# Layer 0 of a four-layer graph kernel: two expert blocks from the first token group, and first products ahead of the last gates

## The chip, the cores and the metric

The kernel runs on one core of a Trainium2 chip. The metric is the device time of one execution in microseconds (us). A forecast and a result are compared by the median of several executions. The engines are TensorE (PE, with PEld for its weight loads), VectorE (DVE), ScalarE (ACT), GpSimd (POOL) and SyncE (SP), which issues most DMAs; each works through its own queue in order.

## The reference

There are 2708 tokens of 256 features. Each of four layers first mixes tokens through an adjacency matrix and then applies a feed-forward part; the change is in layer 0:

```python
x = x + weights(adj) @ (layernorm(x) @ W + B)   # weights: exp(-2 (1/adj - 1)^2) where adj < 1, else 0
xf = layernorm(x)
gate_logits = xf @ Wg + bg                      # 8 experts
top_w, top_i = jax.lax.top_k(gate_logits, 2)    # two experts for each token
top_w = jax.nn.softmax(top_w, axis=-1)
for e in range(8):
    h = gelu(xf @ W1[e] + b1[e])                # 256 -> 1024
    out = out + w_dense[:, e:e+1] * (h @ W2[e] + b2[e])   # 1024 -> 256
x = x + out
```

## The kernel before

Tokens are cut in 22 tiles of 128 rows (the last one has 20), and the tiles in three groups, `GROUPS`: tiles 0 to 8, 9 to 15 and 16 to 21. For each group the kernel makes the **sums** of the mixing step. A loop over `j` loads one row block of the transposed adjacency matrix, as wide as the group (`adrow`, five buffers, on SP's queue); `weigh` turns it into weights with three ScalarE and two VectorE instructions (`wt`, four buffers); TensorE multiplies them with the messages `msg` (L893) into PSUM. When a group's sums are done, VectorE adds them to `x` (L916), and `send` takes the group's tokens through the **gates**. It normalises rows (`stats`, `norm_to`, L187), turns them on TensorE (`turn_to`, L203) and copies them on ScalarE (L204), multiplies by `Wg` (L807), finds the two best experts and their weights (`top2_weights`), works out a place in an expert-sorted list for each of a token's two copies (`route`, L384 to L402) and scatters the copies there with indirect DMAs on GpSimd (L492, into the DRAM tensor `taken0`). Each expert has one part of the list for each group, since a group's counts are known only after its gates. Of the next group's sums, as much as fits lies beside a group's gates.

The **expert blocks** then take 256 list entries of one expert at a time. `blocks` computes on VectorE, from the counts that are known (`known`), which expert (`ei`) and which list entries (`ix`) each block has. Full blocks that the first two groups are certain to fill are called "A" (`NA = 9`), and are found before the last group's gates; "B" and "C" are found after them. `took` says how many full blocks of each expert were used, so that later calls leave them out. An object of class `Blocks` runs them. `fetch` reads the expert's number into a register of SP and loads its weights, `wa` and `wb` (L761, L766); `fetch_rows` gathers the rows (L506, `xs`), behind all scatters that may have written them; `turn` transposes them (L558) and copies them on VectorE (L564, `xTs`). `run` then makes the first products (L591, four instructions for each of 8 slices of the hidden layer), Gelu on ScalarE (L593, `hTs`), the second products (L601, into `yacc`), adds the bias and multiplies by the gate's weight on VectorE (L603, L604), and scatters the result (L492, `given`). There are 24 such blocks in this stage.

The order of work on each engine is made when the program is built: a planner takes the instructions in the order of the program text, puts one that is ready ahead of an earlier one that is not, and adds the waits. The text adds orders of its own where wanted. In the kernel before, the first block's turn is put behind the gates' product of the third-last tile:

```python
work0.run(hc, items, beside, gated[-3])
```

The two first blocks' rows are fetched in the text near the end of the last group's loop (`j == NT - 5`), behind the scatters of the first and the second group, and their weights after that loop:

```python
if end and j == NT - 5:
    past = list(scattered["taken0"])
    items = [(full, b, past, taken[0][: 2 * held], True) for b in range(NA)]
```

Weights are loaded behind the last matrix row that was asked for in the text at that point (`reads[-1]`). The PSUM banks and the SBUF pools of the blocks (`hc`) take the place of those of the sums, tile by tile. The last group's `stats` go by Ln and Exp on ScalarE (`by_log`), those of the other groups by a square root in integer and float steps on VectorE (`rsqrt`, L152 to L163).

Of the kernel before, what the change touches and what calls it, by code (L numbers as in the profile page):

```python
# [36 lines left out]
def rows(t):  # L37
    return min(P, N - t * P)
# [28 lines left out]
def adj_ffn4(ctx: ExitStack, tc: tile.TileContext, a: dict, out: bass.AP):  # L67
# [24 lines left out]
    def ps_acc():  # L92
        return pools["psum"].tile([P, W], F32, tag="acc", name="ps_acc", bufs=pools["acc"])
# [311 lines left out]
    def blocks(pool, brief, known, NB, B, name, done=None, full=False, least=0):  # L405
# [44 lines left out]
        ei = pool.tile([P, NB], I32, name="b_ei", tag="b_ei" + name)  # L450
        v.tensor_scalar(ei, eb[:, :, 0], float(E - 1), None, op0=ALU.min)
        v.tensor_tensor(vec[:, 0, :], nb[:, :, 0], end, ALU.subtract)
        if done is not None:
            v.tensor_tensor(vec[:, 0, :], vec[:, 0, :], done, ALU.add)
        v.tensor_tensor(hot, eb.to_broadcast([P, NB, E]),
                        count[:, None, :E].to_broadcast([P, NB, E]), ALU.is_equal)
        part = brief.tile([P, NB, K, E], F32, name="b_part", tag="b_part" + name, bufs=1)
# [9 lines left out]
        row = pool.tile([P, NB, M], F32, name="b_row", tag="b_row" + name)  # L467
        step = pool.tile([P, NB, M], F32, name="b_step", tag="b_step" + name)
        ix = pool.tile([P, NB, M], I32, name="b_ix", tag="b_ix" + name)
        v.tensor_tensor(row, pos, of[:, :, 1:2].to_broadcast([P, NB, M]), ALU.add)  # L470
        for i in range(1, len(known) - 1):

            v.tensor_tensor(step, pos, of[:, :, 2 * i : 2 * i + 1].to_broadcast([P, NB, M]), ALU.is_ge)
# [1 line left out]
                            ALU.mult)  # L475
            v.tensor_tensor(ix if full and i == len(known) - 2 else row, row, step, ALU.add)
        if full:

            took = pool.tile([P, E], F32, name="b_took")
            v.tensor_scalar(took, vec[:, 0, :], float(NB), None, op0=ALU.add)  # L480
            v.scalar_tensor_tensor(took, took, 0.0, nb[:, :, 0], op0=ALU.max, op1=ALU.min)
# [41 lines left out]
    class Blocks:  # L523
# [4 lines left out]
        def __init__(self, pool, given, weights):  # L528
            self.pool, self.given = pool, given
            self.weights, self.ahead, self.rows, self.at = weights, [], [], [0, 0]  # L530
            self.late = None
            self.ik, self.ok = "taken0", "given0"

        def fetch(self, item):
# [14 lines left out]
                gather(xs[:, k, :], src, ix[:, b, k : k + 1], src.shape[0] - 1, self.ik, past)  # L549
            self.rows.append((xs, ix.shape[2]))  # L550

        def turn(self, pool, rows, after=None):
            xs, n = rows
            xT = pool.tile([P, DC, 2 * P], F32, name="xTs", bufs=2)
            p = pools["psum"].tile([P, W], F32, name="turned", bufs=1)
            for k in range(n):
                for c in range(DC):
                    i = te.transpose(p[:, (c * 2 + k) * P : (c * 2 + k + 1) * P],  # L558
                                     xs[:, k, c * P : (c + 1) * P], ident)
                    if after is not None:  # L560
                        tc.add_manual_dep(i.ins, after, mybir.DependencyInfo(
                            mybir.DependencyClass.NoSync, mybir.DependencyReason.DATA),
                            reason="order")
            v.tensor_copy(xT[:, :, : n * P], p.rearrange("p (c t) -> p c t", c=DC)[:, :, : n * P])  # L564
            return xT

        def run(self, pool, items, during=None, after=None):

            HC = 1024 // P
            self.late = pool  # L570
            ahead, todo, rows_todo = self.ahead, list(items[len(self.ahead):]), list(items[len(self.rows):])
            while rows_todo and len(self.rows) < 3:
                self.fetch_rows(rows_todo.pop(0))
            while todo and len(ahead) < 2:
                self.fetch(todo.pop(0))
            turned = self.turn(pool, self.rows[0], after)
            for n in range(len(items)):
                w1, bias, w2 = ahead.pop(0)
                (xs, m), xT = self.rows.pop(0), turned
                if rows_todo:  # L580
                    self.fetch_rows(rows_todo.pop(0))
# [4 lines left out]
                hT = pool.tile([P, HC, 2 * P], F32, name="hTs", bufs=1)  # L586
                for f in range(HC):
                    if f % 2 == 0:
                        p = ps_acc().rearrange("p (k t) -> p k t", k=2)
                    for c in range(DC):  # L590
                        te.matmul(p[:, f % 2, : m * P], lhsT=w1[:, c, f * P : (f + 1) * P],  # L591
                                  rhs=xT[:, c, : m * P], start=(c == 0), stop=(c == DC - 1))
                    s.activation(hT[:, f, : m * P], p[:, f % 2, : m * P], AF.Gelu,  # L593
                                 bias=bias[:, f : f + 1])
                if self.rows:
                    turned = self.turn(pool, self.rows[0])
                y = pool.tile([P, 2, D], F32, name="ys", bufs=2)
                q = pools["psum"].tile([P, 2, D], F32, name="yacc", bufs=2)
                for k in range(m):
                    for f in range(HC):  # L600
                        te.matmul(q[:, k, :], lhsT=hT[:, f, k * P : (k + 1) * P], rhs=w2[:, f, :],  # L601
                                  start=(f == 0), stop=(f == HC - 1))
                    v.tensor_tensor(y[:, k, :], q[:, k, :], w2[:, HC, :], ALU.add)  # L603
# [146 lines left out]

    NA, MOST = 9, (2 * N + E * (P - 1)) // (2 * P)
    assert NA <= -(-(2 * held - E * (2 * P - 1)) // (2 * P))
    ALWAYS, HALVES = 13, 2
    with ExitStack() as l0:
        hw = l0.enter_context(tc.tile_pool(name="h0", side="right", reuse_waits="tile", bufs=1))
# [14 lines left out]
        hcs, reads, gated, own_rows = [], [], [], []  # L770
# [15 lines left out]
        def send(tiles):  # L786
# [4 lines left out]
            if tiles is GROUPS[-1]:  # L791
                parts = [tiles[:2], tiles[2:]]
            st = {t: (z, t - part[0]) for part in parts
                  for z in [stats(part, by_log=len(parts) > 1)] for t in part}
            xr = (tp if len(parts) == 1 else own_rows[0]).tile(
                [P, GMAX if len(parts) == 1 else G, 2, XW], F32, name="xr", bufs=1)[:, :G]
            lg = tp.tile([P, G, E], F32, name="lg", tag=f"lg{G}", bufs=1)
# [1 line left out]
            for i, t in enumerate(tiles):  # L799
                r = rows(t)  # L800
                norm_to(xr[:r, i, 0, :D], t, st[t][1], st[t][0])
                g.tensor_copy(xr[:r, i, 1, :D], xr[:r, i, 0, :D])
                xT = tp.tile([P, DC, P], F32, name="xT", bufs=2)
                turn_to(xT[:, :, :r], xr[:r, i, 0, :D], r, ps_acc() if len(parts) > 1 else None)
                p = ps_tmp()
                for c in range(DC):
                    made = te.matmul(p[:r, :E], lhsT=xT[:, c, :r], rhs=wg[:, c, :],  # L807
                                   start=(c == 0), stop=(c == DC - 1))
                gated.append(made.ins.name)
# [43 lines left out]
        for tiles in GROUPS:  # L853
# [8 lines left out]
            for j in range(FULL):  # L862
# [33 lines left out]
                if end and j == 2:  # L896
                    cols = [gp.tile([P, GMAX * P], F32, name=name, tag=name, bufs=bufs)[
                        :, : NT * Q].rearrange("p (t c) -> p t c", c=Q)
                            for name, bufs in (("adrow", 5), ("y", 3), ("wt", 4))]
                    last_columns(cols[0])  # L900
                    weigh(*cols, P)
                    last = last_sums(acc[-1].rearrange("p k d -> p (k d)"), cols[2],
                                     lambda j, r: msg[:r, j, :], D)
                    v.tensor_tensor(x[:LAST, FULL, :], x[:LAST, FULL, :], last, ALU.add)
                if end and j == NT - 5:
                    past = list(scattered["taken0"])
                    items = [(full, b, past, taken[0][: 2 * held], True) for b in range(NA)]
                    for item in items[:2]:
                        work0.fetch_rows(item)
            for item in items[:2] if end else ():  # L910
                work0.fetch(item)
            for p, pair in zip(acc, pairs):
                if pair[0] == len(own):
                    continue
# [2 lines left out]
            if end:  # L917
# [5 lines left out]
                hcs.append(hc)  # L923
                own_rows.append(behind_gate.enter_context(
                    tc.tile_pool(name="x0", reuse_waits="tile", bufs=1)))
            send(tiles)
            if tiles is GROUPS[-2]:
                full = blocks(hw, tp, known, NA, 2 * P, "A", full=True)
        rest = blocks(hw, hc, known, MOST - NA, 2 * P, "B", done=full[2], least=P)
        twice = hw.tile([P, E], F32, name="twice")  # L930
        v.tensor_tensor(twice, full[2], rest[3], ALU.add)
# [39 lines left out]
                    ad[: rows(j)], a["adjT"][j * P : j * P + rows(j), c0 : c0 + N // 2]))  # L971
                read.append((j, c0, ad))

        work0.run(hc, items, beside, gated[-3])
        assert not parts and not read
        work0.run_rest(hc, more, left[0])

# [927 lines left out]
```

## Time and profile before

| | us |
|---|---|
| median of 3 runs | 1936.62 |
| lowest and highest | 1930.79, 1938.07 |
| the profiled execution | 1935.32 |
| its span, first to last instruction | 1933.6 |

| engine | busy us | share of the span | instructions |
|---|---|---|---|
| PE | 1827.5 | 95% | 9453 |
| DVE | 1092.7 | 57% | 2439 |
| ACT | 642.1 | 33% | 1461 |
| POOL | 344.5 | 18% | 405 |

The profile is one execution. A matrix product in float32 stands in it as two instructions. Its views are a page with the busy share of each engine in 40 equal slices, windows with busy times and the granted TensorE clock (1.00 is full speed), a timeline of each engine, and lists of who waited for whom: a wait is put down to the releaser that came last. In layer 0 the second group's sums end about 197, the third group's at 257, and the expert blocks last until about 607 us.

### The profile page before, as it was taken

The numbers are of one execution on the slowest core, as the hardware profiler recorded it, in microseconds if no ns is written. First come the engines' busy times: TensorE is split into PE (matmuls) and PEld (weight loads), VectorE is DVE, ScalarE is ACT, GpSimd is POOL, SyncE is SP. The second block draws the span as 40 slices with busy tenths as digits, with TensorE's granted clock in tenths as the row PEclk, the third lists the DMA queues.
The fourth block names the chain that finished last, engine by engine and source line by source line (L and its number), as shares of the span: only waits on it lengthen the run. The fifth ranks groups of instructions, "written<-read, shape, count | busy, mean of one in ns | idle before, by whom it ended". The sixth has DMA issues, their size and how long they took to land.

```text
span 1933.6 us, 25684 instructions
## 1 busy us (share of the span) xinstructions
PE 1827.5 (95%) x9453; PEld 1327.0 (69%) x9453; DVE 1092.7 (57%) x2439; ACT 642.1 (33%) x1461; POOL 344.5 (18%) x405
## 2 busy tenths in 40 slices
PE   7999989999998999999796799999899999999998
PEld 6888778888887888888676678888557732232344
DVE  7776862444333524444441175555354398999897
ACT  7868732222223303122231142223232552031131
POOL 1005263333321002314336300000000000000000
PEclk9999989999998999999898999999899999999999
DMA  8435476887764454535777620000101000000000
GB/s 274 138 114 155 120 273 243 342 311 282 301 254 133 144 151 118 149 106 131 222 243 262 264 75 1 1 1 1 44 1 33 17 1 23 23 12 28 20 20 15
DMA packets 90141, 243.94 MB, mean 126 GB/s; under 512 B 18159, under 2 KB 44823, under 8 KB 80792
## 3 DMA queue, kind: packets, MB, share of 16 engines
q1 hardware_dynamic: 70048, 197.09, 30.9%
q0 software_dynamic: 16960, 42.42, 6.9%
q10 hardware_dynamic: 3000, 2.70, 0.5%
q8 instruction: 78, 1.28, 0.3%
q14 instruction: 55, 0.45, 0.1%
HBM read 216.29 MB, written 28.71 MB: 127 GB/s over the span
## 4 chain that ended last, share of the span: by engine, by line
PE 73%; DMA 12%; DVE 6%; issue 5%; ACT 2%; POOL 2%; SPq 0%; POOLq 0%; DVEq 0%; ACTq 0%
PE num L1803 10%; PE ps_acc L1382 9%; PE acc L1174 8%; PE ps_tmp L357 7%; PE acc L893 7%; PE den L1813 6%; PE ps_acc L591 5%; PE yacc L601 4%; PE ps_tmp L250 4%; DMA given<-ys,xs 4%; PE ps_acc L1566 3%; PE yacc L693 2%; DMA hs<-hid,names 2%; DMA given<-ys,names 1%; PE ps_tmp L203 1%
## 5 line engine op out<-in xcount | busy, mean ns | idle before, releaser
L1773 DVE SCALAR_TENSOR_TENSOR e<-arena,G,mask 128x1024 f32<-128x1024 f32 (+1 forms) x264 | 287.0, 1149 | 13.6 <-PE den L1813 13.6
L1803 PE MATMUL num<-e,wh 128*64 128x512 f32 (+4 forms) x1056 | 215.8, 551 | 0.0
L1382 PE MATMUL ps_acc<-hh,e 128*128 128x257 f32 x882 | 199.2, 382 | 1.7 <-ACT o L1327 1.7
L893 PE MATMUL acc<-msg,wt 128*128 128x256 f32 x882 | 198.5, 382 | 2.0 <-DVE wt L851 1.2
L1174 PE MATMUL acc<-sup,adrow 128*128 128x256 f32 x882 | 198.6, 382 | 1.8 <-DVE adrow L1146 1.8
L893 PEld LDWEIGHTS acc<-msg,wt 128*128 128x128 f32 x882 | 165.6, 191 | 28.0 <-DVE wt L851 2.1
L1174 PEld LDWEIGHTS acc<-sup,adrow 128*128 128x128 f32 x882 | 165.1, 190 | 28.7 <-issue 5.2
L1382 PEld LDWEIGHTS ps_acc<-hh,e 128*128 128x128 f32 x882 | 163.7, 190 | 29.2 <-ACT o L1327 4.3
L591 PE MATMUL ps_acc<-xTs,wa 128*128 128x256 f32 (+1 forms) x768 | 170.6, 375 | 1.0 <-DVE xTs L564 0.8
L593 ACT ACTIVATE hTs<-ps_acc,wa 128x256 f32<-128x256 f32 (+1 forms) x192 | 88.6, 464 | 244.4 <-PE yacc L601 165.6
L601 PE MATMUL yacc<-wb,hTs 128*128 128x256 f32 x736 | 167.4, 380 | 1.9 <-DVE ys L603 1.9
L591 PEld LDWEIGHTS ps_acc<-xTs,wa 128*128 128x128 f32 x768 | 137.6, 191 | 27.3 <-DVE xTs L564 3.8
L1803 PEld LDWEIGHTS num<-e,wh 128*64 128x64 f32 (+1 forms) x1056 | 66.5, 136 | 127.3 <-issue 106.5
L601 PEld LDWEIGHTS yacc<-wb,hTs 128*128 128x128 f32 x736 | 137.6, 190 | 20.2 <-DVE ys L603 2.7
L1376 DVE SCALAR_TENSOR_TENSOR e<-Rb,G,mask 128x640 f32<-128x640 f32 (+2 forms) x110 | 85.1, 775 | 93.1 <-PE ps_acc L1382 93.0
L1813 PE MATMUL den<-e,wh 128*32 128x512 f32 (+4 forms) x1056 | 118.0, 548 | 0.0
L204 ACT COPY xT<-ps_tmp 128x256 f32<-128x256 f32 x98 | 33.6, 364 | 242.5 <-PE ps_tmp L203 217.2
L1143 DVE TENSOR_SCALAR mask<-adrow 128x1024 uint8<-128x1024 f32 (+1 forms) x66 | 41.7, 631 | 124.2 <-DMA adrow<-in_adjT 124.0
L693 PE MATMUL yacc<-wb,hTs 128*128 128x256 f32 x384 | 90.6, 387 | 0.3 <-DMA wb<-in_L_ffn_Wdp 0.3
L851 DVE SCALAR_TENSOR_TENSOR wt<-adrow,wt 128x640 f32<-128x640 f32 (+3 forms) x67 | 71.1, 1063 | 30.6 <-ACT wt L141 30.3
L1813 PEld LDWEIGHTS den<-e,wh 128*32 128x32 f32 (+1 forms) x1056 | 30.2, 108 | 77.9 <-issue 73.8
L492 POOL DMA_INDIRECT given<-ys,xs x46 | 65.9, 1432 | 83.7 <-DVE ys L604 77.9
(452 smaller groups left out, 2570.8 us busy)
## 6 DMA issues: line engine op xcount, KB each, us to landing
adhalf<-in_adjT SPq DMA_DIRECT2D x42, 677.0 KB
wb<-in_L_ffn_W2p SPq DMA_DIRECT2D x24, 1152.0 KB
wb<-in_L_ffn_Wdp SPq DMA_DIRECT2D x24, 1152.0 KB
wa<-in_L_ffn_W1b SPq DMA_DIRECT2D x24, 1028.0 KB
adrow<-in_adjT SPq DMA_DIRECT2D x42, 512.0 KB
adrow<-in_adjT SPq DMA_DIRECT2D x42, 320.0 KB
adrow<-in_adjT SPq DMA_DIRECT2D x21, 576.0 KB
adrow<-in_adjT SPq DMA_DIRECT2D x21, 448.0 KB
```

The source lines that it names most:

```text
L357: te.matmul(p[:, :w], lhsT=w1[:, c, f * P : (f + 1) * P], rhs=xnT[:, c, c0 : c0 + w], start=(c == 0), stop=(c == DC - 1))
L591: te.matmul(p[:, f % 2, : m * P], lhsT=w1[:, c, f * P : (f + 1) * P], rhs=xT[:, c, : m * P], start=(c == 0), stop=(c == DC - 1))
L593: s.activation(hT[:, f, : m * P], p[:, f % 2, : m * P], AF.Gelu, bias=bias[:, f : f + 1])
L601: te.matmul(q[:, k, :], lhsT=hT[:, f, k * P : (k + 1) * P], rhs=w2[:, f, :], start=(f == 0), stop=(f == HC - 1))
L693: te.matmul(q, lhsT=hT[:, f, :], rhs=w2[:, f, :], start=(f == 0), stop=(f == HC - 1))
L893: te.matmul(p[:q, n - pair[0], :], lhsT=wt[:, k : k + q], rhs=msg[:r, j, :], start=(j == 0 and n == pair[0]), stop=(j == FULL - 1 and n == ...
L1174: te.matmul(p[:q, n - pair[0], :], lhsT=ad[:, k : k + q], rhs=sup[:r, j, :], start=(j == 0 and n == pair[0]), stop=(j == FULL - 1 and n == ...
L1376: v.scalar_tensor_tensor(e[:r, :w], Rb[:r, c0 : c0 + w], G[:r, j, :], mask[:r, j, c0 : c0 + w], op0=ALU.max, op1=ALU.mult)
L1382: te.matmul(p[:, : D + 1], lhsT=e[:, k : k + q], rhs=hh[:, j, :], start=(j == 0), stop=False)
L1773: v.scalar_tensor_tensor(e[:, :w], slow[:, m % 2, k, :w], G[:, j, 2 * pair + k, :], mask[:, j, c0 : c0 + w], op0=ALU.max, op1=ALU.mult)
L1803: te.matmul(num[k * DK : (k + 1) * DK, hf, :q], lhsT=wh[some, j, 2 * pair + k, :DK], rhs=e[some, h0 - c0 : h0 - c0 + q], start=(j == 0), s ...
L1813: te.matmul(den[z : z + Q, :q], lhsT=wh[some, i, 2 * pair + k, DK : DK + 1] .to_broadcast([some.stop - some.start, Q]), rhs=e[some, h0 - c ...
```

## The change

There are now two "E" blocks (`N0 = 2`). By counting alone, the first group of 1152 tokens, with 2304 copies over 8 experts, has at least two full blocks of 256. They are found right after the first group's gates. Their rows are fetched at `j == 0` of the last group's loop, behind the first group's scatters alone; their weights at `j == 8` and `j == 14` of that loop. "A" has the seven others of the nine, and leaves out what "E" took.

When the last group's sums are done, the text goes on with the turn and the first products of the first block (`first_products`, cut out of `run`), and only then with the last group's gates, whose transposes are put behind the last one of these products (`at_last`). The last group's `stats` now go by `rsqrt` on VectorE as the others' do. The number of blocks and the work in them are the same. `took` moves up in `blocks` and is made before `done` is added.

```diff
@@ blocks
+        if full:
+            took = pool.tile([P, E], F32, name="b_took", tag="b_took" + name)
+            v.tensor_scalar(took, vec[:, 0, :], float(NB), None, op0=ALU.add)
+            v.scalar_tensor_tensor(took, took, 0.0, nb[:, :, 0], op0=ALU.max, op1=ALU.min)
         if done is not None:
             v.tensor_tensor(vec[:, 0, :], vec[:, 0, :], done, ALU.add)
+            if full:
+                v.tensor_tensor(took, took, done, ALU.add)
...
@@ class Blocks
-        def turn(self, pool, rows, after=None):
+        def turn(self, pool, rows):
...
+        def first_products(self, pool, weights, xT, m):
+            w1, bias, _ = weights
+            hT = pool.tile([P, HC, 2 * P], F32, name="hTs", bufs=1)
+            for f in range(HC):
+                if f % 2 == 0:
+                    p = ps_acc().rearrange("p (k t) -> p k t", k=2)
+                for c in range(DC):
+                    i = te.matmul(p[:, f % 2, : m * P], lhsT=w1[:, c, f * P : (f + 1) * P],
+                                  rhs=xT[:, c, : m * P], start=(c == 0), stop=(c == DC - 1))
+                s.activation(hT[:, f, : m * P], p[:, f % 2, : m * P], AF.Gelu,
+                             bias=bias[:, f : f + 1])
+            self.at_last = i.ins.name
+            return hT
...
-            turned = self.turn(pool, self.rows[0], after)
+            turned = self.begun or self.turn(pool, self.rows[0])
+            self.begun = None
...
+                hT = self.made or self.first_products(pool, (w1, bias, w2), xT, m)
+                self.made = None
...
@@ send
-                  for z in [stats(part, by_log=len(parts) > 1)] for t in part}
+                  for z in [stats(part)] for t in part}
...
+                first = len(nc.cur_bb.bb.instructions)
                 turn_to(xT[:, :, :r], xr[:r, i, 0, :D], r, ps_acc() if len(parts) > 1 else None)
+                for k in nc.cur_bb.bb.instructions[first:] if len(parts) > 1 else ():
+                    if k.engine == mybir.EngineType.PE:
+                        tc.add_manual_dep(k, work0.at_last, mybir.DependencyInfo(
+                            mybir.DependencyClass.NoSync, mybir.DependencyReason.DATA),
+                            reason="order")
...
@@ the loop of the sums
+                if end and j == 0:
+                    items = [(early, b, past0, taken[0][: 2 * held0], True) for b in range(N0)]
+                    for item in items:
+                        work0.fetch_rows(item)
+                if end and j in (8, 14):
+                    work0.fetch(items[j // 6 - 1])
                 if end and j == NT - 5:
                     past = list(scattered["taken0"])
-                    items = [(full, b, past, taken[0][: 2 * held], True) for b in range(NA)]
-                    for item in items[:2]:
-                        work0.fetch_rows(item)
-            for item in items[:2] if end else ():
-                work0.fetch(item)
+                    items += [(full, b, past, taken[0][: 2 * held], True) for b in range(NA - N0)]
...
+                work0.late = hc
+                work0.begun = work0.turn(hc, work0.rows[0])
+                work0.made = work0.first_products(hc, work0.ahead[0], work0.begun, 2)
             send(tiles)
+            if begin:
+                early = blocks(hw, tp, known, N0, 2 * P, "E", full=True)
+                past0 = list(scattered["taken0"])
             if tiles is GROUPS[-2]:
-                full = blocks(hw, tp, known, NA, 2 * P, "A", full=True)
+                full = blocks(hw, tp, known, NA - N0, 2 * P, "A", done=early[2], full=True)
...
-        work0.run(hc, items, beside, gated[-3])
+        work0.run(hc, items, beside)
```

More of the change, by code (lines that the diff above doesn't have):

```diff
@@ L469, in blocks @@
         ix = pool.tile([P, NB, M], I32, name="b_ix", tag="b_ix" + name)
-        v.tensor_tensor(row, pos, of[:, :, 1:2].to_broadcast([P, NB, M]), ALU.add)
+        v.tensor_tensor(ix if full and len(known) == 2 else row, pos,
+                        of[:, :, 1:2].to_broadcast([P, NB, M]), ALU.add)
         for i in range(1, len(known) - 1):
@@ L477, in blocks @@
         if full:
-            took = pool.tile([P, E], F32, name="b_took")
-            v.tensor_scalar(took, vec[:, 0, :], float(NB), None, op0=ALU.add)
-            v.scalar_tensor_tensor(took, took, 0.0, nb[:, :, 0], op0=ALU.max, op1=ALU.min)
             return ei, ix, took
@@ L530, in __init__ @@
             self.weights, self.ahead, self.rows, self.at = weights, [], [], [0, 0]
-            self.late = None
+            self.late, self.begun, self.made = None, None, None
             self.ik, self.ok = "taken0", "given0"
@@ L557, in turn, with run @@
                 for c in range(DC):
[L558 to L563, printed above, removed]
+                    te.transpose(p[:, (c * 2 + k) * P : (c * 2 + k + 1) * P],
+                                 xs[:, k, c * P : (c + 1) * P], ident)
             v.tensor_copy(xT[:, :, : n * P], p.rearrange("p (c t) -> p c t", c=DC)[:, :, : n * P])
             return xT
-        def run(self, pool, items, during=None, after=None):
-            HC = 1024 // P
+        def first_products(self, pool, weights, xT, m):
[11 more added lines that the diff above has]
+            return hT
+        def run(self, pool, items, during=None):
             self.late = pool
@@ L585, in run @@
                     during(n)
[L586 to L594, printed above, removed]
+                hT = self.made or self.first_products(pool, (w1, bias, w2), xT, m)
+                self.made = None
                 if self.rows:
@@ L752, in adj_ffn4 @@
     assert NA <= -(-(2 * held - E * (2 * P - 1)) // (2 * P))
+    held0 = sum(rows(t) for t in GROUPS[0])
+    N0 = 2
+    assert N0 <= -(-(2 * held0 - E * (2 * P - 1)) // (2 * P))
     ALWAYS, HALVES = 13, 2
@@ L768, in weights0 @@
             return wa[:, :2048].rearrange("p (c h) -> p c h", c=DC), wa[:, 2048:], w2
-        hcs, reads, gated, own_rows = [], [], [], []
+        hcs, reads, own_rows = [], [], []
         behind_gate = ExitStack()
@@ L803, in send @@
                 xT = tp.tile([P, DC, P], F32, name="xT", bufs=2)
+                first = len(nc.cur_bb.bb.instructions)
                 turn_to(xT[:, :, :r], xr[:r, i, 0, :D], r, ps_acc() if len(parts) > 1 else None)
+                for k in nc.cur_bb.bb.instructions[first:] if len(parts) > 1 else ():
[3 more added lines that the diff above has]
+                            reason="order")
                 p = ps_tmp()
                 for c in range(DC):
-                    made = te.matmul(p[:r, :E], lhsT=xT[:, c, :r], rhs=wg[:, c, :],
-                                   start=(c == 0), stop=(c == DC - 1))
-                gated.append(made.ins.name)
+                    te.matmul(p[:r, :E], lhsT=xT[:, c, :r], rhs=wg[:, c, :],
+                              start=(c == 0), stop=(c == DC - 1))
                 v.tensor_tensor(lg[:r, i, :], p[:r, :E], bg[:r], ALU.add)
```

## The prediction

> **What bounds the kernel now.** I read the page's slices first, then the busy times in short windows around the end of layer 0's sums, then TensorE's timeline there, then who waited for whom, then the queue of SyncE.
>
> ```profile
> PE   7999989999998999999796799999899999999998
> PEclk9999989999998999999898999999899999999999
> ```
>
> TensorE (PE) is busy in nearly every slice of 48.3 us; the others have room. So the end moves only by what TensorE loses. Slice 6 (241.7 to 290.0 us) shows an 8 in both rows: idle time, and a lowered clock. The windows split it (length, then busy us of PE, PEld, DVE, ACT, POOL, then granted clock, DMA share, GB/s):
>
> ```profile
> 252.00:256.00 4.00, 4.00 (x20) 3.54 (x19) 0.97 (x2) 0.04 (x1) 3.08 (x4) 1.00 1.01 420
> 256.00:260.00 4.00, 1.11 (x6) 0.63 (x4) 3.96 (x15) 0.50 (x2) 0.42 (x1) 1.00 1.02 422
> 260.00:264.00 4.00, 3.56 (x16) 2.77 (x16) 2.16 (x10) 1.52 (x5) 0.49 (x1) 0.59 1.02 419
> 264.00:268.00 4.00, 2.88 (x14) 2.35 (x12) 0.51 (x4) 1.76 (x5) 3.08 (x4) 0.50 0.77 296
> 268.00:272.00 4.00, 3.17 (x14) 2.64 (x15) 1.90 (x8) 0.46 (x1) 3.24 (x5) 0.50 0.37 99
> 272.00:276.00 4.00, 4.00 (x18) 3.39 (x16) 1.75 (x10) 2.81 (x4) 3.09 (x4) 0.70 0.39 109
> ```
>
> The sums end inside the second row; then the clock is lowered. A mean of 0.59 in the third row is 3.3 us at 0.50, two rows are all at 0.50, and 0.70 in the last is 2.4 us: 13.7 us, from about 260.7 to 274.4. TensorE's timeline (start, us, what, and in brackets the idle time before it and its releaser) names the gaps:
>
> ```profile
> 239.68 17.43 PE L893 MATMUL acc<-msg,wt 128*128 128x256 f32 x80
> 260.24 1.14 PE L203 MATMUL ps_acc<-ident,xr 128*128 128x128 f32 x4 [3.13 <-DVE xr L187]
> 268.04 0.90 PE L558 MATMUL turned<-ident,xs 128*128 128x128 f32 x3 [1.17 <-DMA xs<-taken,b_ix]
> 271.02 4.49 PE L591 MATMUL ps_acc<-xTs,wa 128*128 128x256 f32 x12 [0.78 <-DVE xTs L564]
> 288.44 3.72 PE L601 MATMUL yacc<-wb,hTs 128*128 128x256 f32 x16 [1.86 <-DVE ys L603]
> 297.63 0.60 PE L558 MATMUL turned<-ident,xs 128*128 128x128 f32 x4
> 311.90 0.60 PE L558 MATMUL turned<-ident,xs 128*128 128x128 f32 x4
> ```
>
> The sums end at 239.68 + 17.43 = 257.11. Then TensorE waits 3.13 us for the last group's normalised rows, runs the gates at half clock, and waits for the first block's gathered rows, which could not be fetched earlier:
>
> ```profile
> POOL xs L506 <- DMA taken<-xr,r_ix: 7.1, 1, 7.1
> ACT y L141 <- DMA adrow<-in_adjT: 0.6, 2, 0.3
> ```
>
> (the second row, of the stretch 197 to 257, is used below).
>
> **What TensorE loses there.** From 257.11 to 297.63 are 40.5 us. In them lie 64 first products (L591), 32 second products (L601), two turns, six tiles' gates and the route. The steady period is 311.90 - 297.63 = 14.27 us for 64 products and one turn of 0.44 (L558 at 297.63, its follower at 298.07), so 0.216 us a product: 96 cost 20.7, two turns 0.9. A gate tile amid the second group's sums takes 0.62 us (four L807 in 0.36, two L203 in 0.26, at 216.72 to 217.34), six take 3.7. The 16 route products from 230.71 to 232.59 take 1.88, 14 take 1.65. Sum 27.0; lost 13.5 us: 7.1 of idle (3.13 + 0.15 + 1.17 + 0.78 + 1.86), 6.4 of half clock.
>
> **The change part by part.**
>
> Rows and weights of two blocks come early. The first group's scatters are issued by 194.3 and land within 12.6 us at worst; four gathers of 1.02 + 0.30 us follow, 5.3 us of GpSimd, in its 14.4 us wait ahead of the row copies at 211.75. Queued behind them are those copies and the scatters at 234.75, which nobody needs before 263.5. With a landing of 4.5 the rows are there by 217, forty us before use. Cost 0; cover gone, 5.3 us on GpSimd alone. The same four gathers leave GpSimd at 263.5, so block three's rows come earlier.
>
> VectorE: blocks "E" adds some 21 small instructions of about 0.17 us, 3.6 us, near 165 to 175, where every tile of sums leaves it 1.11 us idle (its wait for ACT before L851) and TensorE is full: cost 0, 3.6 if the cover were gone. Three more in "A" (0.16 each) fall near 236, where TensorE has 2 us of weights in stock: 0, at worst 0.5. The last group's square roots move from ScalarE (0.29 + 0.20 twice) to VectorE: 12 instructions of 0.165 in two parts, 4.0 us. They end near 262 to 266, while first products of 32 x 0.216 = 6.9 us run to about 265: 0, at worst 1.0. ScalarE's three table loads of 1.28 us (267.18, 273.63, 275.15) remain three, the first now idle time after 252.04; three banks of ps_acc hold 5.2 us of products over the other two: 0.
>
> First products ahead of the gates. This fills the 3.13 us and the 1.17 us, and a filled TensorE shouldn't drop its clock: in the trace the half clock begins only after the long wait. All 13.5 us are to be had, less three terms.
>
> Term a, the copy of the turned rows ahead of the first product: 0.78 by its row. It is 0 if the turn is put before the sums' end, and 2.0 if it queues on VectorE behind the adds that end at 257.92. I take 0.8, the row of this very wait.
>
> Term b, second products held by L603. VectorE is full from 277 to 290 with the block numbers of "B" and "C", and an in-order L603 in there holds yacc. 1.86 by its row; 0 if the copies come earlier, 5 if two of them are caught. I take 1.9.
>
> Term c, the matrix rows. SyncE's queue now has two sets of weights (1028 + 1152 KB, 2.2 MB) between the rows of the last sums. At 420 GB/s a set takes 5.3 us; three sets from 243.81 to about 266 took 7.3 each beside the scatters. A row issued at 242.70 was used at 246.69, with 0.35 us of waiting: no spare time. TensorE's stock is the time from the last weight (252.89) to the start of its last ten products (257.11 - 2.1 = 255.0): 2.1 us. So a set costs 5.3 - 2.1 = 3.2 if all of it is felt, two 6.4; 0 if the rows ahead of it suffice (DMA is at 0.43 to 0.48 of its time from 208 to 232). ScalarE is idle 3.8 of 12 us from 232 to 244 and can catch up. I take 1.5, nearer to the small waits of the row above.
>
> The sum: 13.5 - 0.8 - 1.9 - 1.5 = 9.3 us. The profiled execution took 1935.32 (span 1933.6), so 1926.0 for it; it lies 1.3 below the median of the runs, 1936.62, and I forecast a median: 1927.3. Behind 297.63 each block follows the last one without idle time up to the layer's end, so the gain isn't given back there. Less than 0.5% (9.7 us) is about what a measurement here can't tell from no change; the runs of before spread over 7.3 us.
>
> [...]
>
> **The rivals.** B, given back on VectorE: the gates end as late as before, so its full stretch stays at 277 to 290; if the first block's L603 stands behind it, TensorE does 72 products, two turns, gates and route, 15.6 + 0.9 + 5.4 = 21.9 us, and stands from 279 until 288.4. Ahead are then only 18 first products, 3.9 us: 1932.7. For it: L603 at 287.97 did just that. Against: its input is ready some 8 us sooner, ahead of the full stretch.
>
> D, the clock falls all the same in the gates: 9.3 - 6.4 = 2.9, 1933.7. Against it: second products lie between the gates now.
>
> C, the slower end: the two sets of weights starve the last sums. At 7.3 us each, and with no stock left, 14.7 us go, against 13.5 - 0.8 - 1.9 = 10.8 won: 1940.5. A wait as long as the 3.13 us also brought 6.4 us of half clock: 1947. It decides from 5.4 us a set. For it: rows without spare time; against: the first set falls where the DMA engines are half idle.
>
> That the change doesn't do what it says would need rows or weights not landed by 257; forty us speak against it.
>
> **How the numbers follow.** Forecast A 0.64, B 0.13, D 0.06, C 0.17. A runs from 13.5 (no term) to 4.1 us won (a 2.0, b and c 3.7 each), about 0.4 of all being above 9.7 us. B, D and the rest of A lie within 0.5%, as does C without the clock. Range: 1936.6 - 13.5 less 3 for the runs' scatter, 1920, up to C without the clock, 1942. Faster 0.41, same 0.43, slower 0.16.
>
> **What would show it.** L591 right behind L893 with under 2 us of idle; a granted clock of 1.00 from 256 to 280; the turn of the third block near 288 rather than 297.63; the sums ending no more than 2 us later than 257.1. Wrong: waits for adrow of over 3 us between 205 and 240, TensorE idle before L893, a wait for L603 over 4 us, or a clock still at 0.50.

## The result

| | us |
|---|---|
| before, median of 5 runs (lowest, highest) | 1935.13 (1930.79, 1938.07) |
| after, median of 5 runs (lowest, highest) | 1925.29 (1923.09, 1928.12) |
| ratio of after to before | 0.9942, 95% interval 0.9925 to 0.9959 |
| the profiled execution of after, and its span | 1928.12, 1926.4 |

The changed kernel is 9.8 us faster, 0.58% with an interval of 0.41 to 0.75%. Two later comparisons with before, on two chips, gave 0.9950 (0.9934 to 0.9965) and 0.9946 (0.9933 to 0.9960). The profiled execution of after is the slowest of its five, 2.8 us above their median, so the two traces are compared stage by stage and not by their spans.

First, from the page of the changed kernel, the slices of TensorE and of its clock:

```profile
PE   7999999999998999999787799999899999999998
PEclk9999999999998999999898899999899999999999
```

The two 8s of slice 6 are gone. The windows of the changed kernel at the end of layer 0's sums (length, busy us of PE, PEld, DVE, ACT, POOL, then granted clock, DMA share, GB/s) show why:

```profile
256.00:260.00 4.00, 2.27 (x13) 1.77 (x11) 3.39 (x10) 0.00 (x0) 1.30 (x3) 1.00 0.34 89
260.00:264.00 4.00, 3.98 (x18) 3.34 (x19) 4.00 (x31) 2.49 (x4) 3.08 (x4) 1.00 0.98 411
264.00:268.00 4.00, 4.00 (x20) 3.25 (x19) 2.73 (x11) 1.90 (x4) 3.38 (x6) 1.00 0.80 291
268.00:272.00 4.00, 4.00 (x31) 3.46 (x30) 0.50 (x3) 2.13 (x6) 2.10 (x6) 1.00 0.86 280
272.00:276.00 4.00, 4.00 (x26) 3.36 (x26) 2.29 (x13) 1.52 (x3) 0.00 (x0) 1.00 0.64 252
```

The granted clock is 1.00 in all five rows, where before it was 0.50 to 0.70 from 260 to 276, and TensorE is full from 260 on. Its timeline in the changed kernel (start, us, what, idle before it and the releaser):

```profile
238.14 19.69 PE L907 MATMUL acc<-msg,wt 128*128 128x256 f32 x90
257.67 0.60 PE L561 MATMUL turned<-ident,xs 128*128 128x128 f32 x4
260.02 2.86 PE L573 MATMUL ps_acc<-xTs,wa 128*128 128x256 f32 x12 [1.75 <-DVE xTs L563]
268.31 0.60 PE L203 MATMUL ps_acc<-ident,xr 128*128 128x128 f32 x4
283.16 0.38 PE L561 MATMUL turned<-ident,xs 128*128 128x128 f32 x2
286.83 0.38 PE L561 MATMUL turned<-ident,xs 128*128 128x128 f32 x2
301.93 0.60 PE L561 MATMUL turned<-ident,xs 128*128 128x128 f32 x4
```

The first block's turn stands right behind the sums, one wait of 1.75 us is left, the gates (L203, L822) run among products, and the third block's turn comes in two halves at 283.16 and 286.83. Since the planner cut that turn in two, the fourth block's turn is the cleaner mark: 301.93 where the kernel before had 311.90, 9.97 us sooner. The last second products of layer 0 start at 594.74 (before: 603.75), 9.01 us sooner:

```profile
594.74 3.19 PE L607 MATMUL yacc<-wb,hTs 128*128 128x256 f32 x14
```

So what was won at 302 us was mostly kept to the end of the layer and of the kernel. Two more traces of the changed kernel (a_after, b_after below) have this line at 593.65 and 594.09: 10.1 and 9.7 us sooner than the one trace of before.

The waits of the changed kernel (engine, line, releaser; us in total, times, longest), the first two between 250 and 300 us and the third between 197 and 257 us, answer the three terms of the sum:

```profile
PE ps_acc L573 <- DVE xTs L563: 1.7, 1, 1.7
PEld yacc L607 <- DVE ys L609: 0.2, 1, 0.2
ACT y L141 <- DMA adrow<-in_adjT: 0.2, 1, 0.2
```

### The profile page after: what moved, and what is told of

Its sections match the earlier page's. It is cut to its first block, busy times and chain, and to the rows that moved or that the text cites. A ratio compares the mean times of both kernels' runs of the same rounds, so it can differ in the third digit from the quotient of the medians.

```text
span 1926.4 us, 25726 instructions
## 1 busy us (share of the span) xinstructions
PE 1825.9 (95%) x9453; PEld 1326.4 (69%) x9453; DVE 1095.6 (57%) x2483; ACT 641.6 (33%) x1457; POOL 342.8 (18%) x405
## 3 DMA queue, kind: packets, MB, share of 16 engines
q8 instruction: 78, 1.28, 0.3%
## 4 chain that ended last, share of the span: by engine, by line
PE 71%; DMA 14%; DVE 6%; issue 4%; ACT 2%; POOL 2%; SPq 0%; POOLq 0%; DVEq 0%; ACTq 0%
PE num L1825 10%; PE ps_acc L1404 9%; PE acc L907 9%; PE acc L1196 8%; PE ps_tmp L357 7%; DMA given<-ys,xs 6%; PE den L1835 5%; PE ps_acc L573 4%; PE ps_tmp L250 4%; PE yacc L607 4%; PE ps_acc L1588 3%; DMA hs<-hid,names 2%; DMA names<-taken,b_ix 1%; DVE e L1795 1%; DMA given<-ys,names 1%
```

## The experiments

The main theory behind them: the stretch behind the sums was thin for TensorE (waits and half clock), and dense products put into it, whose rows and weights are already there, fill it. Three groups were run, each on a chip of its own and each beside the kernel before: a_after with e1 to e3, then e4 to e7, then b_after with e8 to e10. The ratios are to before on the same chip, and an e-kernel's trace is compared with those of its group where there is one of the changed kernel in it. A trace is one execution of several: those of a_after, b_after and e2 are the fastest of their runs, those of e6, e8 and e10 the slowest, so stretches are compared and not whole spans. A useful measure in the traces is the time from the end of the sums to the fourth block's turn: 311.90 - 257.11 = 54.79 us before, 301.93 - 257.83 = 44.10 in the changed kernel.

**a_after: the changed kernel itself.**

> The changed kernel once more, as the measure for the others on this chip. Theory and rival both: 0.992 to 0.996 of before; no half clock from 256 to 280 us; the sums' end near 257.8.

Ratio 0.9950 (0.9934 to 0.9965). The order and the stretch are those of the first trace: 44.10 us again.

**e1_fill: the kernel before, with products that do nothing in the hole.**

```diff
+            last = sums_last[0]
...
+            if len(parts) > 1:
+                last = fill(7, last)            # 14 products of 128x256 behind the sums
...
                 gated.append(made.ins.name)
+                if len(parts) > 1:
+                    last = fill(1, made.ins.name)   # two more behind each gate tile
```

> The kernel before with products of no use (ident times x, never read): 7 of them (14 instructions, 3.0 us) between the last sum and the last group's gates, and one (0.43 us) behind each gate tile. Rows, weights and order of the blocks stay as before. Theory 1, the sum of the prediction, where half clock by itself is worth 6.4 us: the clock stays at 1.00 and the third block's turn comes 5 to 6.4 us sooner, 291 to 293 instead of 297.6, ratio 0.997. Theory 2, the gathered rows bind: they land near 268 whatever the clock, so the wait for them grows from 1.17 us to 3 or 4, only the 12 first products from 271.0 on run faster (4.5 us become 2.6), and the turn comes at most 2 us sooner, ratio 0.999 to 1.000.

Ratio 1.0017 (1.0004 to 1.0030): slower. Lines of its timeline and of its windows:

```profile
258.82 3.18 PE L804 MATMUL ps_acc<-x,ident 128*128 128x256 f32 x14
263.08 0.61 PE L820 MATMUL ps_tmp<-L_ffn_Wg,xT 128*128 128x8 f32 x4 [0.46 <-ACT xT L204]
```

```profile
260.00:264.00 4.00, 3.33 (x18) 2.50 (x17) 3.75 (x17) 1.30 (x5) 0.00 (x0) 1.00 1.03 416
264.00:268.00 4.00, 3.02 (x17) 2.33 (x15) 0.52 (x5) 0.74 (x2) 2.23 (x3) 0.76 0.99 411
```

From the sums' end up to there no wait is longer than 0.46 us, and still the clock went to half at 266.1 us, for 13.7 us. So the prediction's reason, that the half clock begins only after the long wait, is wrong: here it began behind gate tiles with gaps of 0.21 and 0.46 us, with 3.33 of 4 us busy from 260 to 264. Whether a denser filling keeps it away is tried in e8.

**e2_rows_only: the early rows and weights, but the order of before** (the first turn again behind the third-last gate, no products ahead of the gates, the last group's statistics by Ln and Exp).

```diff
-                work0.begun = work0.turn(hc, work0.rows[0])
-                work0.made = work0.first_products(hc, work0.ahead[0], work0.begun, 2)
...
-        work0.run(hc, items, beside)
+        work0.run(hc, items, beside, gated[-3])
```

> The changed kernel with the old order: blocks E, their early rows and weights stay; the last group's gates come first, with statistics by Ln and Exp on ScalarE, and the first block's turn behind the third-last tile's product, as before. Theory 1 (filling TensorE is what counts): 3.13 us idle and the half clock stay, only the 1.17 us go: 1 to 2 us sooner than before, ratio 0.999. Theory 2 (the rows bind): with the rows there, the turn and the first products fit into the gates' waits as the planner puts them, but the fixed order holds the turn to about 267, so 1 to 3 us, ratio 0.9985 to 0.9995. Less than a third of the gain by both.

Ratio 0.9997 (0.9984 to 1.0010). Its timeline has the long wait back, with 13.7 us of half clock behind it; only the wait for the gathered rows is gone:

```profile
260.42 1.01 PE L203 MATMUL ps_acc<-ident,xr 128*128 128x128 f32 x4 [3.14 <-DVE xr L187]
296.33 0.60 PE L561 MATMUL turned<-ident,xs 128*128 128x128 f32 x4
```

The third block's turn is 1.3 us sooner than before; the early rows alone bring no more than that in this trace, and nothing clear in the ratio.

**e3_products_only: the new order, but the rows and weights fetched as before.**

```diff
-                if end and j == 0:
-                    items = [(early, b, past0, taken[0][: 2 * held0], True) for b in range(N0)]
...
-                if end and j in (8, 14):
-                    work0.fetch(items[j // 6 - 1])
```

> The changed kernel without blocks E: first products ahead of the gates, but rows and weights of the first two blocks as before (gathered behind the second group's scatters). Theory 1 (order alone gives most): 0.995 to 0.998. Theory 2 (the rows bind): TensorE has nothing to do from 257 until the rows land near 268, the clock falls, and the gates come behind the first products: 10.9 us idle + 0.8 + 27.0 of work + 2 to 4 at half clock = 41 to 43 us against 40.5 before, ratio 1.000 to 1.002.

Ratio 1.0005 (0.9995 to 1.0015). TensorE stands for the rows, and the clock falls at 259.8 us for 13.7 us:

```profile
266.90 1.11 PE L561 MATMUL turned<-ident,xs 128*128 128x128 f32 x4 [10.55 <-DMA xs<-taken,b_ix]
```

Neither half of the change moves the time by as much as 0.2%; the two together give 0.5%. The gathered rows let the products go ahead, and the products fill the hole.

**e4_gates_bare: the change, with the first block's second products, and the second block's turn, held behind the last gate.**

```diff
+                for k in nc.cur_bb.bb.instructions[first:] if self.gate_last else ():
+                    if k.engine == mybir.EngineType.PE:
+                        tc.add_manual_dep(k, self.gate_last, mybir.DependencyInfo(
```

> The changed kernel with the first block's second products and the second block's turn and first products held behind the last gate tile's product, so that nothing fills the gaps between the gates. Theory 1 (gates by themselves use TensorE too little, and the products between them keep the clock up): half clock for about 13.7 us from some point between 266 and 273, and 4 to 7 us lost against the changed kernel, of which 1 to 3 are waits between gates: half of the gain gone, ratio 0.9965 to 0.998 to before. Theory 2 (only a wait of some 3 us lowers the clock): 1.00 throughout, 1 to 3 us lost, ratio 0.995 to 0.9965.

Ratio 0.9953 (0.9938 to 0.9967). The planner put the six tiles' gates close together, from 269.42 to 273.59, with no product between them and no gap, and the clock stayed at 1.00 until 299.9. Bare gates without gaps did not lower the clock in this trace. But near 296 us TensorE, VectorE and ScalarE all stood still. Windows and timeline:

```profile
268.00:272.00 4.00, 3.42 (x25) 2.97 (x26) 0.33 (x2) 2.05 (x6) 2.51 (x7) 1.00 0.89 304
296.00:300.00 4.00, 0.00 (x0) 0.00 (x0) 0.00 (x0) 0.00 (x0) 2.48 (x3) 0.98 0.83 305
```

```profile
301.25 6.39 PE L608 MATMUL yacc<-wb,hTs 128*128 128x256 f32 x16 [5.67 <-DVE ys L610]
```

VectorE's L610 in turn waited 7.52 us for something that the profile calls only "remote". The traces of e5, e6 and e7, from the same chip, have the same: TensorE idle for 7.00, 7.71 and 5.55 us there, and half clock behind it: 16 products take 6.39, 6.23 and 6.37 us in e4, e5 and e6, against 3.62 at full clock, and 24 take 8.13 us in e7. In the ten other traces, before's among them, nothing like it is seen. The kernel before was 9 to 10 us slower on this chip (median 1947.72, against 1937.90 and 1938.72 on the two others), so it may have it too, but no trace of it was taken there. What it is stays open; the ratios of e4 to e7 are read, the length of their stretch up to the fourth turn is not.

**e5_weights_late: the change, with both early sets of weights asked for only behind the last matrix rows.**

```diff
-                if end and j in (8, 14):
-                    work0.fetch(items[j // 6 - 1])
...
+            for item in items[:2] if end else ():
+                work0.fetch(item)
```

> The changed kernel with the weights of the two E blocks asked for after the loop of the sums, as before. Theory 1 (the matrix rows had time to spare, term c is about 0.7 us or nothing): sums end 0 to 0.7 us sooner, same time as the changed kernel, ratio 0.994. Theory 2 (the early weights cost 1.5 us or more in the sums): 1.5 us or more sooner, ratio below 0.9935. If the first products have to wait for weights instead, 1 to 3 us later.

Ratio 0.9952 (0.9934 to 0.9969). The sums end at 257.19, 0.64 us sooner than in the first trace of the changed kernel, but this says nothing on the weights: three traces of the changed kernel end them at 257.83, 257.68 and 256.83, and they differ already near 198 us, where TensorE waits 1.88, 1.28 and 0.75 us for VectorE's addition to `x`. Measured from the last group's first instruction (L268) to the end of the sums, the stretch in which the early weights travel takes 50.40, 50.40 and 50.39 us in these three, 50.78 in this kernel and 50.79 before. The early weights cost the sums nothing that can be seen.

**e6_turn_early: the change, with the first turn put between the last sums** (18th of 22 rows), in banks and a buffer of its own.

```diff
+                if end and j == 17:
+                    work0.begun = work0.turn(hw, work0.rows[0], True)
...
-                work0.begun = work0.turn(hc, work0.rows[0])
```

> The changed kernel with the first block's turn and its copy put into the sums (text of j = 17, a bank and a tile of their own), so that the first products can follow the last sum at once. Theory 1 (term a is a real wait on TensorE's path): the 1.75 us before the first product go, third block's products 1.5 to 2.0 us sooner than in the changed kernel, ratio to before 0.993. Theory 2 (the gates' rows or VectorE are late next): the time comes back as a wait ahead of the gates, or of yacc, and the ratio stays at 0.994 to 0.995.

Ratio 0.9971 (0.9956 to 0.9985). The wait of 1.75 us is gone, but there is a new one in the gates. Timeline and windows:

```profile
258.75 2.75 PE L573 MATMUL ps_acc<-xT,wa 128*128 128x256 f32 x12
270.91 0.61 PE L822 MATMUL ps_tmp<-L_ffn_Wg,xT 128*128 128x8 f32 x4 [1.50 <-ACT xT L204]
```

```profile
268.00:272.00 4.00, 2.50 (x21) 2.19 (x20) 0.34 (x3) 0.42 (x2) 3.38 (x5) 1.00 0.87 313
272.00:276.00 4.00, 4.00 (x18) 2.86 (x17) 1.06 (x6) 2.07 (x4) 2.35 (x7) 0.58 0.85 308
```

The gates wait for ScalarE's copies of their turned rows, TensorE has 1.5 us idle in one window, and the clock drops to half for 6.8 us. The 1.5 us and half of the 6.8 us are more than the 1.75 us saved in this trace; the interval of the ratio overlaps those of e4, e5 and e7, so the times don't show a loss against them.

**e7_by_log: the change, with the last group's square roots back on ScalarE.**

```diff
-                  for z in [stats(part)] for t in part}
+                  for z in [stats(part, by_log=len(parts) > 1)] for t in part}
```

> The changed kernel with the last group's statistics by Ln and Exp on ScalarE, as before. Theory 1 (the square roots on VectorE cost nothing because first products run meanwhile, and ScalarE can do Ln and Exp before its table for Gelu): no difference to the changed kernel within 1 us, clock 1.00. Theory 2 (the table changes disturb Gelu): two more table loads of 1.28 us ahead of the first Gelu hold ps_acc, 1 to 4 us lost.

Ratio 0.9952 (0.9932 to 0.9972), as e4 and e5, which make the roots on VectorE. Where they are made doesn't show in the time.

**b_after: the changed kernel on a third chip.**

> The changed kernel once more, as the measure for the three kernels beside it. Theory 1 (in the four kernels e4 to e7 TensorE stood for 5.6 to 7.7 us near 295 us, with VectorE and GpSimd released together by something the profile calls remote; it belongs to the chip or the run, not to their edits): if this chip shows it too, it shows it in this kernel as well. Theory 2 (it belongs to their edits): this kernel has no wait over 1 us between 262 and 310 us, as in its two traces so far. Ratio to before 0.993 to 0.997 by both.

Ratio 0.9946 (0.9933 to 0.9960), the stretch 44.09 us, and no wait over 1.74 us from 257 to 310. This leaves the standstill of e4 to e7 to their chip or to their edits as before, since the changed kernel was not run on that chip.

**e8_fill_more: e1 with a dense filling**, two products also between each tile's turn and its gate's products, so that the gaps are covered.

```diff
+                if len(parts) > 1:
+                    last = fill(2, turns[-1].name)
                 p = ps_tmp()
                 for c in range(DC):
                     made = te.matmul(p[:r, :E], lhsT=xT[:, c, :r], rhs=wg[:, c, :],
...
-                    last = fill(1, made.ins.name)
+                    last = fill(2, made.ins.name)
```

> Kernel before with filler products as in e1, but more of them: 7 products of 128x256 right behind the sums, then in each of the six gate tiles two between the turns and the gate's products and two behind them, so that each tile holds some 2.6 us of work with no gap (the products' results go unused). [...] Theory 2 (the clock falls there for another reason, whatever TensorE does, since the gathers move over 400 GB/s at the same time): half clock for 10 us or more from about 262 to 266 us in this kernel too, the fillers then take twice as long, first product after 283 us, and the kernel is 0.3 to 0.8% slower than before.

Ratio 1.0015 (1.0001 to 1.0029). Timeline and windows:

```profile
277.44 1.99 PE L591 MATMUL ps_acc<-xTs,wa 128*128 128x256 f32 x8 [0.80 <-DVE xTs L564]
```

```profile
264.00:268.00 4.00, 4.00 (x26) 3.64 (x25) 0.21 (x2) 0.74 (x2) 2.73 (x3) 1.00 0.96 375
268.00:272.00 4.00, 4.00 (x24) 3.50 (x23) 0.29 (x2) 0.75 (x2) 3.23 (x5) 1.00 0.44 124
```

In the same gates, beside the same gathers, the clock now stays at 1.00, and falls (for 3.4 us, at 282.0) only behind the two waits of 276 to 281 (0.80 and 0.89 us). This speaks against theory 2: from 260 to 264 us the DMA engines moved 421 GB/s here and 416 GB/s in e1. It also weighs the hole: the filling is 14 + 6 x 8 = 62 products of 0.216 us, 13.4 us of added work, and the stretch to the fourth turn grew from 54.79 to 59.12, by 4.3. Some 9 us of the added work cost no time in this stretch.

**e9_copy_act: the change, with the first turn's copy on ScalarE.**

```diff
-                work0.begun = work0.turn(hc, work0.rows[0])
+                work0.begun = work0.turn(hc, work0.rows[0], s.copy)
```

> The change, with the first block's turned rows copied to SBUF by ScalarE, not by VectorE. Theory 1 (the 1.75 us wait of the first product is the copy standing behind the additions and the moments on VectorE; ScalarE does nothing from 256 to 260 us): the first product starts 0.7 to 1.1 us sooner behind the sums' end, near 259.1 us, and the third block's turn as much sooner; ratio to before 0.001 below that of the changed kernel at most, which the interval can't tell. Theory 2 (the wait is the copy's own time and the route from engine to engine): the first product starts as late as in the changed kernel or later, 1.7 us or more behind the sums' end.

Ratio 0.9945 (0.9924 to 0.9966), not to be told from b_after. In the timelines of ScalarE and of TensorE:

```profile
258.83 0.58 ACT L563 COPY xTs<-turned 128x512 f32<-128x512 f32 x1 [5.75 <-PE turned L561]
259.46 2.86 PE L573 MATMUL ps_acc<-xTs,wa 128*128 128x256 f32 x12 [0.67 <-ACT xTs L563]
```

The wait is 0.67 us, not 1.74, and the stretch 43.02, not 44.09: 1.07 us, as theory 1 said, and too little for the clock on the whole kernel to show.

**e10_one_block: the change with one early block.**

```diff
-    N0 = 2
+    N0 = 1
...
-                if end and j in (8, 14):
-                    work0.fetch(items[j // 6 - 1])
+                if end and j == 8:
+                    work0.fetch(items[0])
```

> The change with one early block, not two: the first block's rows and weights come during the sums, the second block's with the first gathers behind them (near 259 us). Theory 1 (it is the first block's products alone that fill the stretch of the gates; the second block's rows are wanted only near 262.7 and 283 us): the second block's turn waits no more than 2 us for its rows, the clock stays 1.00, ratio to before within 0.001 of the changed kernel's. Theory 2 (the second early block is needed): TensorE waits 3 us or more for the second block's rows or weights between 268 and 290 us, and the kernel loses half of the gain or more (ratio 0.9975 or above).

Ratio 0.9960 (0.9946 to 0.9974), between the two theories. Its trace has the wait of theory 2, but the ratio is not as high as that theory has it. TensorE waits for the second block's rows, and half clock follows from 265.6 for 6.8 us. Timeline and window:

```profile
267.51 0.66 PE L561 MATMUL turned<-ident,xs 128*128 128x128 f32 x2 [4.35 <-DMA xs<-taken,b_ix]
268.00:272.00 4.00, 4.00 (x11) 3.19 (x11) 0.00 (x0) 0.85 (x2) 3.17 (x4) 0.50 0.38 103
```

The stretch to the fourth turn is 50.82 us, so 6.7 of the 10.7 us are lost there, while the medians are only 4.1 us apart (1930.67 and 1926.53), with intervals that overlap. The traced execution took 1938.75 us, 8.1 more than the median of its kernel, so the others may have lost less. The second early block bridges the time until gathers issued behind the sums have landed.

## Why the prediction was right, and where its steps were not

**The hole, 13.5 us, and that it can be filled: right.** The stretch to the fourth turn shrank by 54.79 - 44.10 = 10.69 us. With the one wait left (1.75), 13.5 - 1.75 = 11.75 were to be had; the other 1.06 lie in small pieces, among them gates that cost about 4.05 us for six tiles (268.31 to 273.66 less six products) where 3.7 were put.

**"A filled TensorE shouldn't drop its clock": right in its use, wrong in its reason.** In e1 the clock fell with no wait over 0.46 us ahead of the fall; in e8, with the gaps filled, it stayed at 1.00 from 256 to 280. So rival D, a clock that falls in the gates all the same, was a nearer danger than the 0.06 it got: e6 is just that, with 1.5 us of idle time in the gates and 6.8 us of half clock. What kept the changed kernel from it is not shown. Right behind its sums, with the wait of term a in it, TensorE was busy for 2.27 of 4 us (2.25 and 2.26 in a_after and b_after), less than the 2.50 ahead of the fall in e6, and the clock stayed at 1.00. Whether a wait of 2.0 us there, the bound that the prediction gave term a, would have brought the half clock, no run shows. With the copy on ScalarE (e9) TensorE was busy for 3.33 of these 4 us.

**Term a, the copy ahead of the first product: 0.8 put, 1.75 measured,** inside its bounds. It was priced by the row of the same wait before, with VectorE free; in its new place the copy queues behind the last additions and moments. The lines of VectorE in the changed kernel:

```profile
257.64 1.00 DVE L932 TENSOR_TENSOR x<-x,acc 128x512 f32<-128x512 f32 x2
258.56 0.18 DVE L177 BATCH_NORM_AGGREGATE mv<-st 128x2 f32<-128x6 f32 x1
258.65 0.72 DVE L176 BATCH_NORM_STATS2 st<-x 128x6 f32<-128x256 f32 x2
259.29 0.68 DVE L563 COPY xTs<-turned 128x512 f32<-128x512 f32 x1
```

The turn is done near 258.3, the copy starts at 259.29. e9 confirms it: without this queue the wait is 1.07 us shorter.

**Term b, second products held by L603: 1.9 put, 0 measured.** L609 (its name in the changed kernel) runs at 275.84 and 281.78 without TensorE waiting. The reason weighed under rival B as speaking against it holds for the first of the two: its input is ready ahead of VectorE's full stretch, which lasts here from about 280 to 291. The second one runs within that stretch, and TensorE meanwhile has other products to do.

**Term c, matrix rows behind weights: 1.5 put, nothing measured.** The waits on `adrow` are 0.2 us in all, and the last group's stretch is 0.39 us shorter than before. The weights travelled beside the rows (327 GB/s in the window 208 to 220, 329 from 232 to 244) and ScalarE hardly waited; rival C needed 5.4 us a set.

**The terms priced at nothing: right.** The early gathers ran on GpSimd from 195.11 to 200.5, in its wait ahead of 212.86. TensorE is full from 160 to 196 us (36.00 of 36 us busy) beside the new blocks' numbers on VectorE. The square roots are done at 264.56, while first products run to 268.3. One detail was wrong: ScalarE's first table load for Gelu does not lie in idle time but at 261.23, behind the first products; no wait of TensorE for it shows.

**The sum.** Terms a, b and c came to 4.2 us and were in fact 1.75 - 0.39 = 1.36; the small pieces took 1.06, and the last group of this one trace began 1.11 us later (207.43 against 206.32). Ahead of it TensorE waited 1.88 us near 198, where before had 0.85, and the clock was at half for 3.4 us from 199.7 (0.86 in the window 196 to 208, against 1.00 before), in the place of a wait of 1.15 us before; a_after and b_after have no half clock there. 13.5 - 1.36 - 1.06 - 1.11 = 9.97 at the fourth turn, where 9.3 were predicted. The closeness of 9.8 to 9.3 in the medians is thus partly luck, errors of size that cancel. The forecast of 1927.3 stands against 1925.29 also because before is 1.5 us lower in five runs than in three. And the interval of the gain, 7.9 to 14.5 us, can't tell the terms apart: the traces alone do.

**Not given back: right.** 9.0 to 10.1 us at the end of layer 0 in three traces, 9.8 in the medians. Which parts carry it was not asked by the prediction's sum: it could be read as two gains, early rows and filled gates, that add up. e2 and e3 show that each alone is worth nothing that can be told.

## What to carry to other kernels

Where an engine that sets the end runs thin between two stages, look for dense work of the next stage whose input can be known early, and move the data and the work together; e2 and e3 show that either alone may measure as nothing. Price the one wait that stays by what is queued ahead of it at its new place, not by its row at the old one. Then read the granted clock of that stretch in a trace, and don't conclude it from the longest wait: in e1, with no wait over 0.46 us ahead of it, the half clock lasted 13.7 us, as long as behind the wait of 3.13 us before.

## What the runs showed of the hardware that was not expected

The granted clock fell in e1 at 266.1 us, after 3.9 us of gate tiles with gaps of 0.2 to 0.5 us each, in e6 after a window with 2.50 of 4 us busy (268 to 272), and in e5 at 273.7 us, behind a wait of 0.82 us among the gates. It stayed at 1.00 in e4 through 4.2 us of transposes and 128x8 products without gaps (269.42 to 273.59), in e8 with the gaps filled (3.80 to 4.00 of 4 us busy in each window from 260 to 276), and in the changed kernel behind a window with 2.27 of 4 us busy (256 to 260). So neither the longest wait nor the busy share of a window sorts these cases: the clock fell with waits of at most 0.46 us in e1 and stayed up behind one of 1.75 us in the changed kernel, and it fell behind 2.50 of 4 us busy and stayed up behind 2.27.

The half clock that followed was not of one length either: 13.7 us before and in e1, e2 and e3, 6.8 in e6 and e10, and 3.4 in e5 and e8. What decides when it begins and how long it lasts, these runs don't show.
